# Three sums in another order, one more buffer, and two moved steps in a planned graph-network kernel

## Chip, cores and metric

The kernel runs on one core of one Trainium2 chip. The metric is the device time of one execution in microseconds (us). The kernel before took 2420.64 us in the median of three runs (2420.32 to 2423.39); the execution that the profiler recorded took 2417.17 us.

## What is computed

There are 128 graphs of 128 nodes with 512 features each. Two layers follow each other, both with a residual sum and a layer norm; all is float32.

```python
# layer 0: graph attention with 8 heads of 64 units
feats = einsum('bnf,hfu->bhnu', X, W)
dense = leaky_relu(e_self[..., :, None] + e_neigh[..., None, :], 0.2)
att = softmax(dense + NEG_BIG * (1.0 - A), axis=-1)
out = relu(einsum('bhij,bhju->bhiu', att, feats) + b)
x = layernorm(x + out)
...
# layer 1: hypergraph convolution, twice, with the incidence H = (adj != 0)
w = adj[:, 0, :]                       # the first row of the adjacency
Dn = 1 / einsum('nce,ne->nc', H, w)    # node scale
Be = 1 / H.sum(axis=1)                 # edge scale
conv(x, W) = Dn * (H @ (Be * (H.T @ (x @ W.T)))) + b
h = layer_norm(relu(conv(x, W1)))      # 512 -> 1024
y = conv(h, W2)                        # 1024 -> 512
x = layernorm(x + y)
```

## The kernel before

**Pairs and stages.** The work goes in 64 pairs of graphs (`PAIRS`), `p` from 0. Each pair passes through stages that are spread over five periods (`lag` 0 to 4): loads and masks first, then the features of the attention, the attention itself, the hidden layer h, and the output. In a steady period the engines work on several pairs at once, each in another stage.

**The order of the work is written by hand.** Every step has a planned time inside a period of `T = 38.6` planned units: `at(lag, time, fn, ...)` puts a step at `(p + lag) * T + time`. All steps of all pairs, and those of the prologue in `todo` (L1138), are sorted by this time (L1232) and issued in that order. So a planned time sets only the order in which an engine, or a DMA queue, gets its instructions. The tables `first` (L1161) and the one for the last pairs (L1219) give single steps other times. Each engine takes its instructions strictly in this order, and waits by itself where data or a buffer isn't ready. PE is TensorE, DVE is VectorE, ACT is ScalarE, POOL is GpSimd, and SP is SyncE, which issues most DMAs.

**Seven products instead of eight.** The three large multiplications (`chain`, L325: pf are features, ph the hidden layer, py the output) multiply blocks of two by two with seven products, which need sums of blocks of both operands. PE takes the products in the order 1, 2, 6, 5, 7, 4, 3. Products 1, 6, 7 and 4 add up in bank X, 2 in bank Y, 5 and 3 in bank W. ACT copies X after products 1, 6 and 7 into the buffers 0, 1 and 2 (`copy`, L340; the pf and py copies share buffers), and the results are sums of such a copy and Y or W: `f_sum` (L502), `h_sum` (L862) and `y_sum` (L925). Product 3 adds to W, so it waits until the DVE sum that reads W after product 5 is done.

**The h sums.** For py, the operand sums are made by POOL from h: `h_sums` (L909) calls `first_sums` (L458), one instruction of 128x512 each. With h[g] the halves of graph g of the pair:

```python
        in0, in1, op = (
            (a[1][0], a[1][1], ALU.add), (t[:, 0], a[0][0], ALU.subtract),
            (a[0][0], a[1][0], ALU.subtract), (a[0][1], t[:, 1], ALU.subtract),
        )[i]
```

Sum 0 takes h alone, sum 1 takes sum 0, sum 2 takes h alone, and sum 3 takes sum 1. Before the change POOL makes them in the order 2, 0, 1, 3. In `rows_product` (L479) product 6 takes sum 1, product 7 sum 2, product 5 sum 0 and product 3 sum 3. On POOL, `rstds` "o" and the three `squares` of graph 0 (L899) stand ahead of them, and the three `squares` of graph 1 behind. On PE, product 6 of py (planned 27.7) stands right behind `attend_pair` (L692, 64 small matmuls into pav), which multiplies the transposed attention eT. Half of eT is made by the second pair of `e_transpose` (L635) on DVE, planned at 21.5 and 21.55.

**The f sums.** Three of the four `f_sum` steps are on DVE: (0, 0) adds copy 0 and Y (planned 18.2), (1, 1) adds copy 2 and W (21.4), (0, 1) adds copy 1 and W after product 3 (24.4). (1, 0) is an ACT copy of X. Between 18.2 and 21.4 DVE has no other step.

**The first rows.** `load_first_row` (L108) brings w, the first row of the adjacency of both graphs, spread over all partitions, with two DMAs on SP. `nodes` (L353) multiplies it in place on DVE and writes node scales by way of `dn` and `dr`; `write_nodes` (L371) stores `dr` to DRAM (`dd_d`) and `spread_nodes` (L572) reads it back spread (`dnb`), for `r_evict` (L448, R). The tile w has one buffer. In the prologue `load(3)` is planned at 143.1, and `nodes` of pair 2 at 149.8, so that the load of pair 3's w stands in the SP queue before the step that uses pair 2's. Behind it on SP stand `load_rows` (x), `write_sums`, `read_sums` (149.77), `write_nodes` and `spread_nodes` of pair 2.

**The squares' sums.** The variance of h is summed over the partitions by way of DRAM: `sum_blocks` (L946, DVE) makes `sr`, `write_sums` and `read_sums` store it (`sd`) and read it back (`sums_out`), and `sum_rest` (L971, DVE) adds the rest. `h_rstd` (POOL, L997) makes the scale of `y_scale` (DVE, L1004), and `output` (PE, pq) follows it.

**The weight sums of the prologue.** `second_sums` (L221) makes four sums of blocks of W2 once. t1 and t2 are POOL's (planned 126.5), t3 (`slice(2, 3)`, b22 - b12) is DVE's at 123.15, t4 DVE's at 141.0. Around t3 on DVE stand `r_evict` of pair 1, a maximum of pair 1, `h_sum` (1, 1) of pair 0 (126.55) and `scale_edges` of pair 2 (126.6).

Of the kernel before, what the change touches and what calls it, by code (L numbers as in the profile page):

```python
# [8 lines left out]
F32 = mybir.dt.float32  # L9
# [11 lines left out]
def kernel(  # L21
# [45 lines left out]
    nc = tc.nc  # L67
    G, N, F = x.shape
    P = 128
# [14 lines left out]
    work = ctx.enter_context(tc.tile_pool(name="work", bufs=1))  # L84
# [22 lines left out]

    def load_first_row(p):  # L108
        s = st[p]
        s["w"] = work.tile([P, 2, N], F32, tag="w", name=f"w_{p}")  # L110
        for g in range(2):
            nc.sync.dma_start(s["w"][:, g, :], adj[2 * p + g, 0, :].partition_broadcast(P))

    def load(p):
        load_adj(p)
        load_first_row(p)
# [195 lines left out]
    LAST = PAIRS - 1  # L312
# [9 lines left out]
    def at(lag, time, fn, *args, since=0, until=PAIRS):  # L322
        steps.append((lag, time, fn.__name__, range(since, until), fn, args))
# [168 lines left out]
    def feature(s, i, to, start):  # L492
# [4 lines left out]
          feature, FW, since=2)  # L497
# [9 lines left out]
        else:  # L507
            nc.vector.tensor_tensor(dst, by_head(s["pf", i]), by_head(s["pf", where]), op=ALU.add)

    at(1, 18.2, f_sum, 0, 0, 0, "Y", since=2)  # L510
    at(1, 21.4, f_sum, 1, 1, 2, "W", since=2)
    at(1, 24.4, f_sum, 0, 1, 1, "W", since=2)
    at(1, 23.4, f_sum, 1, 0, None, "X", since=2)
# [395 lines left out]
    def h_sums(p, s, i):  # L909
        first_sums(s, "hS", f"hS_{p}", halves(s["h"], KH // 2), i, nc.gpsimd, "hS")  # L910

    at(3, 20.9, h_sums, 0, until=LAST)
    at(3, 22.2, h_sums, 1, until=LAST)
    at(3, 19.6, h_sums, 2, until=LAST)
    at(3, 23.4, h_sums, 3, until=LAST)


# [1 line left out]
    def weigh(s, i, to, start):  # L919
# [3 lines left out]
          QU, 1, until=LAST)  # L923
# [198 lines left out]
    for t, fn, *args in (  # L1122
# [18 lines left out]
        (13.05, prepare_vectors, ()),  # L1141
        (14.05, load_weights, (nc.scalar, w1_blocks[:2], w1t, F // 2, HALF)),
        (12.95, load_first_row, (1,)),
        (15.46, load_weights, (nc.sync, w1_blocks[:1:-1], w1t, F // 2, HALF)),
        (16.1, everywhere, (b2_bc, b2, nc.sync)),
# [7 lines left out]
        (117.8, prepare_output_blocks, (slice(2, 3),)),  # L1153
        (118.1, prepare_output_blocks, (slice(3, 4),)),
        (126.5, prepare_output_block_sums, (nc.gpsimd, slice(0, 2))),
        (123.15, prepare_output_block_sums, (nc.vector, slice(2, 3))),
        (141.0, prepare_output_block_sums, (nc.vector, slice(3, 4))),
        (100.0, prepare_mean_columns, ()),
    ]
# [116 lines left out]
```

## Time and profile before

| what | value |
|---|---|
| median of three runs | 2420.64 us (2420.32 to 2423.39) |
| profiled execution | 2417.17 us |
| its span, first to last instruction | 2415.4 us |
| granted TensorE clock, mean over the span | 0.997 |
| one steady period, from product 6 to product 6 of the next pair (1223.26 to 1259.96) | 36.70 us |
| busy in a steady period (1186.57 to 1223.26): PE, DVE, POOL, ACT | 36.59, 32.22, 28.48, 23.73 us |
| PE busy in the first 150 us | 127.61 us |
| PE busy in the last 116 us | 105.65 us |
| HBM | 142 GB/s over the span |

A group of instructions in the profile is named by line, engine, operation and the tiles that it writes and reads (`pyX<-w_sb,hS`: product into py's bank X, from weights and h sums). PE is the matmul side of TensorE and PEld its weight loads, which overlap the matmuls; their ends are modelled, so that a PE "busy" without a gap can hide a short stall, and the distance from start to start is the better measure. Nearly all PE work has line 97, the helper `columns`, so groups are told apart by their tiles. "idle" in a timeline is the time in which the engine did nothing before the group, and the name behind it is what ended this. SPq is the queue of SP: its times are those at which DMAs are issued, not those at which they land.

### The profile page before, as it was taken

The numbers are of one execution on the slowest core, as the hardware profiler recorded it, in microseconds if no ns is written. First come the engines' busy times: TensorE is split into PE (matmuls) and PEld (weight loads), VectorE is DVE, ScalarE is ACT, GpSimd is POOL, SyncE is SP. The second block draws the span as 40 slices with busy tenths as digits, with TensorE's granted clock in tenths as the row PEclk, the third lists the DMA queues.
The fourth block names the chain that finished last, engine by engine and source line by source line (L and its number), as shares of the span: only waits on it lengthen the run. The fifth ranks groups of instructions, "written<-read, shape, count | busy, mean of one in ns | idle before, by whom it ended". The sixth has DMA issues, their size and how long they took to land.

```text
span 2415.4 us, 81039 instructions
## 1 busy us (share of the span) xinstructions
PE 2374.1 (98%) x32309; PEld 1880.3 (78%) x32309; DVE 2083.3 (86%) x4456; ACT 1524.0 (63%) x4481; POOL 1830.5 (76%) x2060
## 2 busy tenths in 40 slices
PE   7899999999999999999999999999999999999998
PEld 5677887877877878778878778778777777787776
DVE  7888889889888888898898898898888888888875
ACT  4565765756756656657657567567566576575663
POOL 5787787787777777877877877877778777777774
PEclk9999999999999999999999999999999999999999
DMA  6445545445455555454455454555554545545541
GB/s 196 131 132 157 146 142 155 139 143 153 148 144 148 147 147 149 142 154 143 139 154 147 140 151 145 143 149 146 149 147 141 153 141 140 149 139 147 149 120 45
DMA packets 432872, 347.10 MB, mean 144 GB/s; under 512 B 153176, under 2 KB 382064, under 8 KB 432496
## 3 DMA queue, kind: packets, MB, share of 16 engines
q1 hardware_dynamic: 429024, 337.46, 48.5%
q8 instruction: 255, 4.18, 0.7%
q10 hardware_dynamic: 3472, 4.47, 0.6%
q14 instruction: 121, 0.99, 0.2%
HBM read 239.08 MB, written 102.73 MB: 142 GB/s over the span
## 4 chain that ended last, share of the span: by engine, by line
PE 49%; DVE 22%; POOL 16%; DMA 5%; ACT 4%; issue 2%; SPq 1%; POOLq 0%; DVEq 0%; ACTq 0%
PE pyX L97 13%; PE phX L97 9%; POOL hS L468 8%; PE pyW L97 8%; POOL sq L903 5%; DVE o L804 4%; PE pz L97 4%; PE phY L97 4%; PE pyY L97 4%; DVE h L865 3%; DVE statso L758 2%; ACT nb L604 2%; DVE o L1023 2%; DVE hB L434 2%; DVE nm L610 1%
## 5 line engine op out<-in xcount | busy, mean ns | idle before, releaser
L343 ACT COPY py<-pyX 128x257 f32<-128x257 f32 x189 | 70.8, 374 | 540.2 <-PE pyX L97 523.8
L97 PEld LDWEIGHTS phX<-zS,w_sb 128*64 128x64 f32 x6144 | 345.1, 137 | 40.5 <-POOL ft L741 21.0
L97 PE MATMUL phX<-zS,w_sb 128*64 128x128 f32 x6144 | 368.5, 273 | 3.5 <-ACT ph L343 3.5
L903 POOL TENSOR_TENSOR sq<-sq 128x512 f32<-128x512 f32 (+2 forms) x384 | 344.3, 897 | 20.1
L588 POOL TENSOR_TENSOR nb<-nb,neg 128x512 f32<-128x512 f32 x256 | 320.3, 1286 | 29.9 <-DMA nb<-rd 29.0
L604 ACT ACTIVATE nb<-nb,ft 128x128 f32<-128x128 f32 x1020 | 325.3, 392 | 17.9 <-POOL nb L588 17.7
L618 ACT ACTIVATE nb<-nb,nm 128x128 f32<-128x128 f32 x1024 | 319.6, 390 | 12.1 <-DVE nm L610 12.0
L766 POOL TENSOR_TENSOR rso<-veo,mhalf 128x2 f32<-128x2 f32 x63 | 44.2, 702 | 337.9 <-DVE veo L764 337.9
L97 PE MATMUL pyX<-w_sb,hS 128*64 128x257 f32 x2016 | 243.3, 382 | 7.2 <-POOL hS L468 1.7
L97 PE MATMUL pyX<-w_sb,h 128*64 128x257 f32 x2016 | 240.3, 379 | 0.5 <-ACT py L343 0.5
L880 ACT ACTIVATE h<-h,vecs 128x128 f32<-128x128 f32 x768 | 239.1, 393 | 2.4 <-DVE h L865 1.7
L97 PE MATMUL pyW<-w_sb,hS 128*64 128x256 f32 x2016 | 239.5, 379 | 0.0
L610 DVE TENSOR_REDUCE nm<-nb 128x4 f32<-128x512 f32 x256 | 175.3, 685 | 41.0 <-ACT nb L604 38.3
L741 POOL TENSOR_TENSOR ft<-ft,b_bc 128x512 f32<-128x512 f32 x128 | 200.7, 1588 | 5.2 <-ACT ft L532 5.2
L97 PEld LDWEIGHTS pyX<-w_sb,h 128*64 128x64 f32 x2016 | 146.0, 137 | 73.9 <-ACT py L343 0.9
L97 PEld LDWEIGHTS pyW<-w_sb,hS 128*64 128x64 f32 x2016 | 144.4, 136 | 73.9 <-issue 0.3
L97 PEld LDWEIGHTS pyX<-w_sb,hS 128*64 128x64 f32 x2016 | 139.5, 136 | 79.8 <-POOL hS L468 15.2
L639 DVE STREAM_TRANSPOSE eT<-eb 128x512 f32<-128x512 f32 x252 | 163.7, 686 | 1.3 <-DMA eb<-ed 0.8
L1006 DVE SCALAR_TENSOR_TENSOR y<-y,rsh,bw_bc 128x512 f32<-128x512 f32 x126 | 150.1, 1229 | 13.7 <-POOL rsh L1002 13.7
L891 ACT ACTIVATE sq<-h 128x512 f32<-128x512 f32 x256 | 160.6, 628 | 2.1
L468 POOL TENSOR_TENSOR hS<-h 128x512 f32<-128x512 f32 x126 | 159.0, 1281 | 0.0
L804 DVE SCALAR_TENSOR_TENSOR o<-y,b_bc 128x512 f32<-128x512 f32 x128 | 158.5, 1277 | 0.0
(178 smaller groups left out, 5563.2 us busy)
## 6 DMA issues: line engine op xcount, KB each, us to landing
nb<-rd SPq DMA_DIRECT2D x127, 512.0 KB
ed<-nb SPq DMA_DIRECT2D x126, 512.0 KB
eb<-ed SPq DMA_DIRECT2D x504, 128.0 KB
x<-in_x_dram SPq DMA_DIRECT2D x64, 512.0 KB
out_dram<-o SPq DMA_DIRECT2D x63, 512.0 KB
xb<-in_x_dram SPq DMA_DIRECT2D x248, 128.0 KB
a<-in_adj_dram SPq DMA_DIRECT2D x64, 128.0 KB
w<-in_adj_dram SPq DMA_DIRECT2D x128, 64.0 KB
```

Source lines behind the costliest of these rows:

```text
L97: nc.tensor.matmul(to[rows], lhs[:, rows], rhs, start=start, stop=stop, skip_group_check=True)
L468: engine.tensor_tensor(t[:, i], in0, in1, op=op)
L588: nc.gpsimd.tensor_tensor(t, t, neg[:, :, None, :].to_broadcast([P, NB, HH, B]), op=ALU.add)
L604: nc.scalar.activation(t, t, AF.Prelu, bias=s["ft"][:, g, h, 0:1], alpha=SLOPE)
L610: nc.vector.tensor_reduce(s["nm"][:, g, hs], scores(p, s, g, hs).rearrange("p b h j -> p h b j"), AX.XY, ALU.max, negate=True,)
L618: nc.scalar.activation(t, t, AF.Exp, bias=s["nm"][:, g, h:h + 1])
L639: nc.vector.transpose(s["eT"][:, g, hs, :].rearrange("p h (b i) -> p h b i", b=NB), s["eb", g][:, :, hs, :].rearrange("p b h j -> p h b j"),)
L741: nc.gpsimd.tensor_tensor(t, t, b0_bc.rearrange("p (h u) -> p h u", h=H), op=ALU.add)
L804: nc.vector.scalar_tensor_tensor(s["o"][:, g, :], s["y"][:, g, :], 2.0, b2_bc, op0=ALU.mult, op1=ALU.add)
L880: nc.scalar.activation(dst[:, k, :], src[:, k, :], AF.Relu, bias=b1_sb[:, c:c + 1])
L891: nc.scalar.activation(s["sq"][:, g, q * KH // 2:(q + 1) * KH // 2, :], hid(s, g, q), AF.Square, scale=DH ** -0.5,)
L903: nc.gpsimd.tensor_tensor(t[:, :n, :], t[:, :n, :], t[:, n:2 * n, :], op=ALU.add)
```

## The change

Four edits; none changes what is computed, and no instruction is added or taken out.

1. The h sums get planned times so that POOL makes them in the order 0, 1, 2, 3 instead of 2, 0, 1, 3.
2. The tile w has two buffers instead of one (one more KB in each partition).
3. `f_sum` (0, 0) moves from 18.2 to 21.45, so that on DVE it comes right after `f_sum` (1, 1) instead of right before it.
4. t3 of the weight sums moves from 123.15 to 126.57, behind `h_sum` (1, 1) of pair 0 and ahead of `scale_edges` of pair 2.

```diff
-        s["w"] = work.tile([P, 2, N], F32, tag="w", name=f"w_{p}")
+        s["w"] = work.tile([P, 2, N], F32, tag="w", name=f"w_{p}", bufs=2)
...
-    at(1, 18.2, f_sum, 0, 0, 0, "Y", since=2)
+    at(1, 21.45, f_sum, 0, 0, 0, "Y", since=2)
     at(1, 21.4, f_sum, 1, 1, 2, "W", since=2)
     at(1, 24.4, f_sum, 0, 1, 1, "W", since=2)
     at(1, 23.4, f_sum, 1, 0, None, "X", since=2)
...
-    at(3, 20.9, h_sums, 0, until=LAST)
-    at(3, 22.2, h_sums, 1, until=LAST)
-    at(3, 19.6, h_sums, 2, until=LAST)
+    at(3, 19.6, h_sums, 0, until=LAST)
+    at(3, 20.9, h_sums, 1, until=LAST)
+    at(3, 22.2, h_sums, 2, until=LAST)
     at(3, 23.4, h_sums, 3, until=LAST)
...
-        (123.15, prepare_output_block_sums, (nc.vector, slice(2, 3))),
+        (126.57, prepare_output_block_sums, (nc.vector, slice(2, 3))),
```

## Prediction

> **What bounds the kernel now.** I read the page first, then the list of waits, then each engine's timeline over one steady pair of graphs (1200 to 1260 us), then the same over the prologue (0 to 160 us). The page shows TensorE (PE) busy nearly all the time, and yet its chain of waits spends half the span elsewhere:
>
> ```profile
> PE 2374.1 (98%) x32309; PEld 1880.3 (78%) x32309; DVE 2083.3 (86%) x4456; ACT 1524.0 (63%) x4481; POOL 1830.5 (76%) x2060
> PE 49%; DVE 22%; POOL 16%; DMA 5%; ACT 4%; issue 2%; SPq 1%; POOLq 0%; DVEq 0%; ACTq 0%
> ```
>
> A chain that leaves PE and comes back has to return through a PE wait, however short. The list of waits (total us, times, longest) names it; the second line matters further down:
>
> ```profile
> PEld pyX L97 <- POOL hS L468: 15.2, 58, 0.3
> DVE so L973 <- DMA sums_out<-sd: 63.8, 38, 4.0
> ```
>
> The timelines (start, length, work, count, idle before) place it. PE's weight load first, GpSimd's (POOL) sums second:
>
> ```profile
> 1220.90 2.12 PEld L702 LDWEIGHTS pav<-ft,eT 128*64 128x64 f32 x64
> 1223.26 1.50 PEld L97 LDWEIGHTS pyX<-w_sb,hS 128*64 128x64 f32 x16 [0.25 <-POOL hS L468]
> ```
> ```profile
> 1219.34 2.51 POOL L468 TENSOR_TENSOR hS<-h 128x512 f32<-128x512 f32 x2
> 1221.93 1.28 POOL L468 TENSOR_TENSOR hS<-hS,h 128x512 f32<-128x512 f32 x1
> ```
>
> The first two POOL sums are 2 and 0, the third is sum 1, which product 6 takes. It ends at 1223.21, and PE begins to load it at 1223.26. In pair 0 the sum was just in time, and nothing was lost:
>
> ```profile
> 73.47 2.14 PEld L702 LDWEIGHTS pav<-ft,eT 128*64 128x64 f32 x64
> 75.50 1.53 PEld L97 LDWEIGHTS pyX<-w_sb,hS 128*64 128x64 f32 x16
> ```
>
> From load to load this is 2.03 us in pair 0 and 2.36 in the steady pair: the wait costs **0.33 us**, its 0.25 plus the overlap with the work ahead that is lost. The matmuls agree: attention product, then product 6, from start to start 1.86 + 1.75 us in pair 0, 2.14 + 1.80 steady, again 0.33. All other groups of the steady period follow each other at one fixed distance in nearly every pair (36.70 us from pair to pair). So PE bounds it, with one hole per pair.
>
> The prologue has a larger hole. SyncE's queue and PE there:
>
> ```profile
> 78.91 0.37 SPq L106 DMA_DIRECT2D a<-in_adj_dram  x1
> 87.02 1.27 SPq L112 DMA_DIRECT2D w<-in_adj_dram  x2
> 88.81 0.47 SPq L959 DMA_DIRECT2D sd<-sr  x1
> 93.89 2.67 SPq L965 DMA_DIRECT2D sums_out<-sd  x4
> 96.66 0.38 SPq L373 DMA_DIRECT2D dd_d<-dr  x1
> 98.59 0.38 SPq L575 DMA_DIRECT2D dnb<-dd_d  x1
> ```
> ```profile
> 104.55 3.35 PE L97 MATMUL pq<-y,R 128*64 128x512 f32 x8 [4.12 <-DVE y L1006]
> ```
>
> The load of w for pair 3 stands from 79.3 to 87.0, until `nodes` of pair 2 (VectorE, DVE, 85.14 to 86.99) is done with the only buffer. Behind it wait the squares' sums (`sd`, ready at 85.21) and all that follows them.
>
> **What the Trainium skill says.** "TensorE: Matmul & The Clock Gate", section "What a matmul computes" and its table, lets PE pull weight loads ahead of running matmuls; the trace agrees (loads start 0.08 to 0.1 us before the loads ahead end, and the wait removes this). The same page, "Part 1: The HAM clock gate", has PE at half clock after about 3.4 us of idleness; here too: pq takes 3.35 us after 4.12 idle, 1.89 in the steady pair. "DMA: Bandwidth & Descriptors", section "Anatomy of one DMA", says that waits are held by the issuing sequencer, and that completion costs about 2 us: SP's stall above is such a wait, and dd_d, issued at 96.66, frees DVE at 98.67, 2.0 us later.
>
> **The change, part by part.**
>
> (1) Order of the h sums. Nothing is added; three POOL instructions change places inside an unbroken run, so what stands before and behind them keeps its time. Sum 1 moves from third to second, 1.28 us earlier; sum 2 moves to third and ends at 1223.2, while product 7 that takes it starts at 1226.80, or 1226.47 with the hole gone: 3.2 us spare. The margin at product 6 becomes 1.28 - 0.33 = 0.95 us. Next late is DVE: the second transposes (L639) end at 1220.95, the attention product starts at 1221.12. In pair 0 they ended 0.07 before its start, with no loss; where they were later (pair 53, 0.19 us after the start), its fifth matmul started 0.145 us after their end, and its undisturbed place is 0.115 after the start. So up to 0.03 before the start is free: the margin is 0.17 - 0.03 = **0.14 us**. It is needed only if DVE doesn't follow PE; but DVE's run up to there starts from PE's ph products (ACT's copy at 1204.66), so it moves along. Gain 58 x 0.33 = **19.1 us** (58 times in the list of waits). Pair 62 already has the order 0, 1, 2.
>
> What is taken back: the trip of the squares' sums through DRAM. From the end of L954 to L973 it takes 6.25 to 10.48 us over the 62 pairs; where above 8.74, the pair grew by just the excess (9.37: 37.33 us; 10.48: 38.44). The hole lies inside this allowance, so it shrinks to 8.74 - 0.33 + 0.14 = 8.55. Summed over the trips, the excess rises from 7.4 to 9.3 us: 2.0. In some ten of the same pairs the mask additions wait for nb (24 waits, 29.0 us) and push ACT's copies of zT; I put 0.1 each, 1.0. Together **-3.0**; the bounds are 0 (these pairs overlap) and -6 (each counted twice).
>
> (2) Two buffers for w. In steady pairs w is free 27 us of planned time before its next load: nothing. In the prologue w of pair 3 goes out at 79.3, the x load behind it at 80.3, sd at 85.24 instead of 88.81. The later pairs with slow DMAs had some 4.6 us from sd to the first read: read at 89.8, four of them to 92.4; dd_d at 92.4 instead of 96.66, dnb at 94.4 instead of 98.59. So the wait of `nodes` 3 for dd_d (3.68 us) goes, L973 comes at 95 instead of 98.88, and R, which waits for dnb until 103.25, at 99.0. y_scale then ends near 100.2, as PE ends product 7 (98.48 + 1.75 = 100.2): pq starts at 100.3 instead of 104.55. PE isn't idle for 4 us any more and keeps its clock, another 1.4. Next late is ACT's third ph copy, behind DVE's maxima: product 4 at 102.8 instead of 107.71. DVE, 4.2 to 4.7 us earlier, sets the attention product of that pair. I take **4.5**; 2.0 if sd's trip stays slow behind the x load (its write is 5 us behind it), 5.7 if DVE's waits all close. Not below nothing: no transfer is added, and each is issued earlier.
>
> (3) f sums swapped on DVE. The one for W runs 0.34 us earlier, the one for Y (0.41 us) as much later. PE takes W again at 1220.23, with the sum done at 1219.74: no wait now. Where DVE is late (pairs with 0.33 us at this place) the transposes behind the sums, not moved, are late as well, so the attention product gives the gain back. Cost: ACT's py copy, which takes the buffer that the Y sum reads, starts at about 1219.80 instead of 1219.56; the ft copy behind it waits 0.52 for PE, which covers it. Without that cover, 0.24 per pair. I take **0**, bounds -1 and +1 for all pairs.
>
> (4) The weight sum (L225, 1.28 us on DVE at 61.42) goes behind one h_sum, and PE's third product, which waits 1.54 us for that h_sum, starts 1.2 earlier. But ACT, full from 61.5 to 69, sets when pf is copied; PE waits there again (69.26, 0.38 now). ACT's own shift is 0.1. I take **0**, bounds 0 and +0.3. t3 is first needed by product 7, 15 us later.
>
> Sum: 19.1 - 3.0 + 4.5 = **20.6 us**. The profiled execution took 2417.17 us (span 2415.4): 2396.6. The median of the three runs is 3.5 above it, so 2420.6 - 20.6 = **2400**.
>
> **Rivals.** (A) Part of the hole moves to the next late engine. If DVE's transposes don't come with PE, the hole shrinks by their margin alone: 58 x 0.14 = 8.1, with 4.5: 2408. For it: 0.14 us is little. Against: the chain above ties DVE to PE. (B) The reorder doesn't do what it says, as another sum or another wait ends at the same time; only the prologue gains: 2416. Against: sum 0 and sum 1 both come earlier and POOL has no idle time in the run. (C) Slower: the sums' trip through DRAM becomes the bound. In the last eleven pairs before 2301 us trips averaged 9.2 us, 0.75 us each above the allowance of 8.55. If all 60 were so, 45 us would be paid instead of 7.4: 38 - 23.6 = +14, 2435. It decides from 41 such pairs of 60 on ((23.6 + 7.4) / 0.75); there were eleven. The timed runs' 3 to 6 us above the profiled one may be four to eight more of them.
>
> **How the numbers follow.** About 0.2%, 4.8 us, is what can be told from no change. Forecast 0.73, its own range 2392 (5.7 in the prologue, nothing taken back, 1 from the swap: 25.8, and 3 for the spread of runs) to 2406 (-6, 2.0, -1: 14.1). A 0.19, B 0.05, C 0.03. Reaching into A gives 2392 to 2409. Faster 0.92 (forecast and A), same 0.05 (B), slower 0.03 (C).
>
> **What would show it.** (1) No PEld wait on hS; 36.37 us from pair to pair; the chain almost all PE. (2) w at 79 us behind a; pq in the prologue without idle time and under 2 us long. (3) ACT's py copy 0.2 later, its ft copy unmoved. (4) PE's third product earlier, and a longer wait after it. I am wrong if PE's period stays above 36.5 in the pairs from 400 to 1800 us, or if the sums' trips grow.

## The result and the profile after

The changed kernel takes 2392.13 us in the median of four runs (2391.45 to 2395.00). The kernel before, run beside it on the same chip, takes 2420.48 us (four runs, 2420.04 to 2423.39). The ratio is 0.9883, with a 95% interval from 0.9865 to 0.99: **28.35 us faster**, where 20.6 us and 2400 us were forecast. The profiled execution of the changed kernel took 2395.00 us, with a span of 2393.2; before it was 2415.4. So the two profiled executions lie 22.2 us apart. The remaining 6 us lie between the profiled executions and the other runs: before, the median stands 3.3 us above the profiled one, and after, 2.9 us below it.

The page of the changed kernel, busy times and the chain of work that ended last:

```profile
PE 2359.4 (99%) x32309; PEld 1986.4 (83%) x32309; DVE 2079.3 (87%) x4456; ACT 1529.5 (64%) x4481; POOL 1827.5 (76%) x2060
PE 81%; DMA 7%; DVE 5%; ACT 2%; POOL 2%; SPq 2%; issue 1%; DVEq 0%; POOLq 0%; ACTq 0%
```

The chain now stays on PE for 81% of the span instead of 49%. PE was busy 98% of the time already, so this number could not show the hole. The share of the chain could.

The list of waits of the changed kernel (total us, times, longest) has no line any more in which PE's loads wait for the h sums. The first line below is new in its size (12.2 us before), the second was 63.8 us before, the third 29.0:

```profile
ACT py L343 <- DVE ft L508: 65.9, 58, 1.4
...
DVE so L973 <- DMA sums_out<-sd: 49.0, 36, 3.4
...
POOL nb L588 <- DMA nb<-rd: 30.4, 25, 5.1
```

The steady period of the changed kernel, POOL's sums and then PE's weight loads (start, length, work, idle before):

```profile
1213.61 1.28 POOL L468 TENSOR_TENSOR hS<-h 128x512 f32<-128x512 f32 x1
1214.97 1.27 POOL L468 TENSOR_TENSOR hS<-hS,h 128x512 f32<-128x512 f32 x1
1216.20 1.28 POOL L468 TENSOR_TENSOR hS<-h 128x512 f32<-128x512 f32 x1
1217.44 1.28 POOL L468 TENSOR_TENSOR hS<-h,hS 128x512 f32<-128x512 f32 x1
```
```profile
1215.16 2.14 PEld L702 LDWEIGHTS pav<-ft,eT 128*64 128x64 f32 x64
1217.19 1.53 PEld L97 LDWEIGHTS pyX<-w_sb,hS 128*64 128x64 f32 x16
```

Sum 1 is the second line and ends at 1216.24. Product 6 begins to load it at 1217.19, 2.03 us behind the load of the attention product, the distance that pair 0 had before. The margin is 0.95 us. From pair to pair it is 36.367 us in the median of the start-to-start distances, instead of 36.705. Taken from group to group on PE, in the median of 38 steady pairs, the attention product is 0.28 us shorter and product 6 0.05 us; every other distance is the same to 0.003 us.

The prologue of the changed kernel, SP's queue and then PE:

```profile
80.14 0.37 SPq L106 DMA_DIRECT2D a<-in_adj_dram  x1
80.56 1.92 SPq L112 DMA_DIRECT2D w<-in_adj_dram  x2
...
86.57 0.33 SPq L959 DMA_DIRECT2D sd<-sr  x1
89.65 2.66 SPq L965 DMA_DIRECT2D sums_out<-sd  x4
92.42 0.38 SPq L373 DMA_DIRECT2D dd_d<-dr  x1
93.90 0.38 SPq L575 DMA_DIRECT2D dnb<-dd_d  x1
```
```profile
101.58 1.92 PE L97 MATMUL pq<-y,R 128*64 128x512 f32 x8
```

The load of w goes out right behind that of a, `sd` 2.2 us earlier than before although this run reached product 6 of pair 0 1.3 us later, and pq follows without idle time in 1.92 us instead of 3.35. The granted clock of PE, recorded as 0.5 from 104.0 to 107.4 us before, is 1.0 there now. From product 6 of pair 0 to that of pair 1 it takes 40.30 us, before 45.77.

**Where the 22.2 us went**, in sums worked out from the starts in the trace: 60 periods of 0.338 us less are 20.3; the first period, from product 6 of pair 0 to that of pair 1, is 5.5 shorter; the pairs that run longer than the median cost 9.7 us beyond it instead of 7.4 (I call this their excess), so -2.3; and the run reached product 6 of pair 0 1.3 us later (76.89 against 75.55), so -1.3. Together 22.2.

### The profile page after: what moved, and what is told of

It is laid out like the page before. It is cut to its first block, busy times and chain, and to the rows that moved or that the text cites. A ratio compares the mean times of both kernels' runs of the same rounds, so it can differ in the third digit from the quotient of the medians.

```text
span 2393.2 us, 81039 instructions
## 1 busy us (share of the span) xinstructions
PE 2359.4 (99%) x32309; PEld 1986.4 (83%) x32309; DVE 2079.3 (87%) x4456; ACT 1529.5 (64%) x4481; POOL 1827.5 (76%) x2060
## 3 DMA queue, kind: packets, MB, share of 16 engines
q8 instruction: 256, 4.19, 0.7%
## 4 chain that ended last, share of the span: by engine, by line
PE 81%; DMA 7%; DVE 5%; ACT 2%; POOL 2%; SPq 2%; issue 1%; DVEq 0%; POOLq 0%; ACTq 0%
PE phX L97 16%; PE pyX L97 15%; PE pfX L97 8%; PE phW L97 8%; PE pyW L97 7%; PE phY L97 4%; PE pq L97 4%; PE pfW L97 4%; PE pav L702 4%; PE pz L97 4%; PE pyY L97 4%; DMA nb<-rd 3%; PE pfY L97 2%; DMA rd<-rows 1%; DMA ed<-nb 1%; ACT nb L604 1%
## 5 line engine op out<-in xcount | busy, mean ns | idle before, releaser
L604 ACT ACTIVATE nb<-nb,ft 128x128 f32<-128x128 f32 x1020 | 325.1, 392 | 19.4 <-POOL nb L588 19.4
L97 PEld LDWEIGHTS pyX<-w_sb,h 128*64 128x64 f32 x2016 | 166.4, 136 | 53.5 <-ACT py L343 0.9
L97 PEld LDWEIGHTS pyW<-w_sb,hS 128*64 128x64 f32 x2016 | 168.1, 136 | 50.1 <-issue 0.3
L97 PEld LDWEIGHTS pyX<-w_sb,hS 128*64 128x64 f32 x2016 | 161.9, 136 | 43.8
L804 DVE SCALAR_TENSOR_TENSOR o<-y,b_bc 128x512 f32<-128x512 f32 x128 | 164.0, 1320 | 0.0
```

What stands on the lines that cost most here:

```text
L97: nc.tensor.matmul(to[rows], lhs[:, rows], rhs, start=start, stop=stop, skip_group_check=True)
L604: nc.scalar.activation(t, t, AF.Prelu, bias=s["ft"][:, g, h, 0:1], alpha=SLOPE)
L804: nc.vector.scalar_tensor_tensor(s["o"][:, g, :], s["y"][:, g, :], 2.0, b2_bc, op0=ALU.mult, op1=ALU.add)
```

## The experiments

The theory was the prediction's, and the rivals were those of the prediction and, later, several on the pairs that run longer. All times are medians, and each ratio is to the kernel before on the same chip, in the same set of runs: 2425.16 us for e1 to e4, 2427.88 for e5 to e8, 2427.28 for e9 to e12.

### One part at a time

**e1_h_order_only**: of the change, only this.

```diff
-    at(3, 20.9, h_sums, 0, until=LAST)
-    at(3, 22.2, h_sums, 1, until=LAST)
-    at(3, 19.6, h_sums, 2, until=LAST)
+    at(3, 19.6, h_sums, 0, until=LAST)
+    at(3, 20.9, h_sums, 1, until=LAST)
+    at(3, 22.2, h_sums, 2, until=LAST)
```

> Of the four edits only the order of the h sums (0, 1, 2, 3). Theory (the hole of 0.33 us per pair at product 6 is the main gain): 36.37 us from pair to pair in undisturbed pairs, no PEld wait on hS, 18 to 22 us faster than before, no gain in the prologue, where SP still waits until 87 us with the load of w. Rival (a good part of the 28 us comes from the swapped f sums or the moved weight sum): less than 15 us faster.

Measured: 2404.86 us, 0.9916 (0.9901 to 0.9931), 20.3 us faster. The period is 36.367 us. The hole of the prologue is still there, and larger in this run:

```profile
106.77 3.68 PE L97 MATMUL pq<-y,R 128*64 128x512 f32 x8 [5.58 <-DVE y L1006]
```

So the order makes the whole of the steady gain by itself.

**e2_w_buffers_only**: of the change, only `bufs=2` for w.

```diff
-        s["w"] = work.tile([P, 2, N], F32, tag="w", name=f"w_{p}")
+        s["w"] = work.tile([P, 2, N], F32, tag="w", name=f"w_{p}", bufs=2)
```

> Of the four edits only the two buffers for w. Theory: about 5 us faster, all of it before 125 us: pq of the prologue starts without idle time; the steady period stays at 36.70 us. Rival (what is won in the prologue is lost again at the next wait on hS): 0 to 2 us.

Measured: 2418.61 us, 0.9975 (0.9965 to 0.9985), 6.5 us faster. The period stays at 36.70, and PE's line at the same place of the prologue is

```profile
100.75 1.92 PE L97 MATMUL pq<-y,R 128*64 128x512 f32 x8
```

**e3_f_swap_only**: of the change, only this.

```diff
-    at(1, 18.2, f_sum, 0, 0, 0, "Y", since=2)
+    at(1, 21.45, f_sum, 0, 0, 0, "Y", since=2)
```

> Of the four edits only the two f sums swapped. Theory: within 1 us of before; ACT's py copy starts about 0.24 us later, nothing else moves. Rival (the swap shortens the DMA trips of late pairs, as PE's product 3 isn't held and the spread rows go out earlier): 2 to 6 us faster.

Measured: 2425.70 us, 1.0005 (0.9995 to 1.0015). PE's loads for bank W of the features wait 1.2 us in all (5 times, 0.2 at most) instead of 3.6 (8 times, 0.6 at most), and the attention product waits for DVE instead (1.8 us, 6 times; the list of before has no such wait).

**e4_t3_moved_only**: of the change, only this.

```diff
-        (123.15, prepare_output_block_sums, (nc.vector, slice(2, 3))),
+        (126.57, prepare_output_block_sums, (nc.vector, slice(2, 3))),
```

> Of the four edits only the weight sum t3 moved behind one h_sum. Theory: within 0.5 us of before, as PE's third product starts 1.2 us earlier and PE then waits as much longer for ACT's pf copies. Rival: 1.2 us faster.

Measured: 2426.90 us, 1.0005 (0.9996 to 1.0013). PE's third product starts without a wait, and then PE waits 0.47 and 0.48 us for two copies of pf: the gain is handed back at once.

The four parts give 20.3 + 6.5 - 0.5 - 1.7 = 24.6 us, all together 28.4 and, measured again below, 29.8. The two parts that do nothing have 1 inside their intervals (2.0 to 2.4 us to each side), so this is additive to within a few us.

### Is it the order, and what is the next margin?

**e5_sum1_third**: the changed kernel, but POOL makes the sums in the order 0, 2, 1, 3. Sum 1 is third again, with another sum ahead of it.

```diff
-    at(3, 20.9, h_sums, 1, until=LAST)
-    at(3, 22.2, h_sums, 2, until=LAST)
+    at(3, 22.2, h_sums, 1, until=LAST)
+    at(3, 20.9, h_sums, 2, until=LAST)
...
-                    ("squares", 0): 26.5, ("squares", 1): 26.6, ("h_sums", 2): 22.3,
+                    ("squares", 0): 26.5, ("squares", 1): 26.6, ("h_sums", 2): 22.1,
```

> The changed kernel with the h sums in the order 0, 2, 1, 3: sum 1 is third again, as before the change, and the other three edits stay. Theory (only the place of sum 1 counts): the PEld wait on hS is back with about 0.25 us in each pair, the period is 36.70 us again, some 20 us slower than the changed kernel (5 to 7 us faster than before). Rival (it was the early sum 2 that cost something, or the run as a whole): within 5 us of the changed kernel.

Measured: 2416.66 us, 0.9959 (0.9944 to 0.9974), some 20 us slower than the changed kernel by the ratios (0.9878 for e9 below). The period is 36.588 us, not the 36.70 that had been expected: 0.12 us of the hole are missing, and of the expected waits of 0.25 us in each pair the list shows 21, of 0.2 us at most. The loads in this kernel's steady period:

```profile
1218.03 2.12 PEld L702 LDWEIGHTS pav<-ft,eT 128*64 128x64 f32 x64
1220.28 1.50 PEld L97 LDWEIGHTS pyX<-w_sb,hS 128*64 128x64 f32 x16
```

From load to load it is 2.25 us, between the 2.03 without a hole and the 2.36 with it. In the order 2, 0, 1 sum 1 reads what the instruction right ahead of it wrote, and POOL starts it 0.07 to 0.08 us after that one's end (1214.89 to 1214.97 in the lines after, where the independent sum behind it starts 0.04 us before the end). In the order 0, 2, 1 there is one instruction between the two. So the place of sum 1 makes most of the hole and its dependence on its neighbour the rest. Both point to sum 1 and to no other wait. Of the 20 us, 60 periods of 0.22 us make 13; most of the rest is the excess of the longer pairs (15.5 us against 10.0 in e9), which has another cause, shown below.

**e6_pool_spare_256** and **e7_pool_spare_512**: the changed kernel with one more POOL addition ahead of the h sums of each pair, with 256 columns in the first and 512 in the second. Its result is not used.

```diff
+    spare = const.tile([P, F], F32, name="spare")
+
+    def extra(p, s, engine, n):
+        engine.tensor_tensor(spare[:, :n], b0_bc[:, :n], b2_bc[:, :n], op=ALU.add)
+
+    at(3, 19.5, extra, nc.gpsimd, 256, until=LAST)
```

> The changed kernel with one spare GpSimd addition of 128x256 (about 0.7 us) in each pair ahead of the h sums; its result is used by nothing. Theory (margin of 0.95 us at product 6): no PEld wait on hS, period 36.37 us, within 3 us of the changed kernel. Rival (the margin isn't there): 0.3 us or more per pair, 18 us.

> The same with a spare addition of 128x512 (about 1.27 us), again used by nothing. Theory: 1.27 - 0.95 = 0.32 us beyond the margin, so that the wait of before is back: period 36.69 us, about 19 us slower than the changed kernel. Rival (margin larger, or the spare work falls into POOL's idle time): period 36.37 us.

Measured: 2397.26 us, 0.9874 (0.9858 to 0.9891), and 2413.52 us, 0.9941 (0.9926 to 0.9956). With 256 columns POOL comes 0.73 us later, the period is 36.374, and PE does not wait. With 512 columns it comes 1.275 us later, and the old hole is back. The waits and the loads of e7:

```profile
PEld pyX L97 <- POOL hS L468: 15.4, 58, 0.4
```
```profile
1222.80 2.12 PEld L702 LDWEIGHTS pav<-ft,eT 128*64 128x64 f32 x64
1225.16 1.50 PEld L97 LDWEIGHTS pyX<-w_sb,hS 128*64 128x64 f32 x16 [0.24 <-POOL hS L468]
```

Again 2.36 us from load to load, and a period of 36.707. Of the 1.275 us, 0.34 reach PE, so the margin was 1.275 - 0.34 = 0.93 us, where the prediction had 0.95. By the ratios e7 is some 15 us slower than the changed kernel (0.9941 against 0.9878), where 19 had been expected; its excess is smaller, 7.6 us.

**e8_dve_spare_264**: the changed kernel with the same kind of spare addition on DVE, ahead of the second transposes of eT, to measure the margin of 0.14 us there.

```diff
+    at(1, 21.46, extra, nc.vector, 264, since=3)
```

> The changed kernel with one spare DVE addition of 128x264 (about 0.34 us) in each pair from pair 3 on, between the f sums and the second transposes of eT; its result is used by nothing. Theory (DVE's margin at the attention product is 0.14 us): PE waits there for DVE eT, the period grows by 0.34 - 0.14 = 0.20 us to 36.57, 12 us in all. Rival (DVE has no margin): 0.34 us, 20 us. Second rival (DVE has the same slack as POOL): nothing.

Measured: 2452.45 us, 1.0104 (1.0089 to 1.0119); the period is 37.43 us, 1.06 more, where 0.20 had been expected. That was a miss in the size of the probe. All of the 1.06 us stands in the attention product; every other distance on PE is that of the changed kernel to 0.001 us. DVE, PE and POOL of this kernel at the same moment:

```profile
1199.62 0.42 DVE L508 TENSOR_TENSOR ft<-pf,pfY 128x264 f32<-128x264 f32 x1
1199.96 1.24 DVE L912 TENSOR_TENSOR spare<-b_bc 128x264 f32<-128x264 f32 x1
1201.13 1.29 DVE L639 STREAM_TRANSPOSE eT<-eb 128x512 f32<-128x512 f32 x2
```
```profile
1202.57 1.97 PE L702 MATMUL pav<-ft,eT 128*64 128x65 f32 x60 [0.84 <-DVE eT L639]
```
```profile
1199.65 1.27 POOL L468 TENSOR_TENSOR hS<-h 128x512 f32<-128x512 f32 x1
1200.99 1.35 POOL L468 TENSOR_TENSOR hS<-hS,h 128x512 f32<-128x512 f32 x1
```

The f sum has the same 264 columns, with one operand in PSUM, and takes 0.42 us. The spare has both in SBUF and takes 1.24: it starts at 1199.96 inside a POOL sum that runs to 1200.92, and ends some 0.3 us after it. The Trainium skill says this in "SBUF — State Buffer", section "Who interferes with whom": a DVE instruction with two SBUF inputs contends with a GpSimd instruction that reads SBUF; the ports that the two share are held by one of them at a time, and the order of issue decides which one is blocked. The trace agrees: in all 61 pairs the spare takes 1.23 to 1.25 us and ends 0.29 us after that POOL sum. The transposes came 1.17 us later (1201.13 after 1199.96) and PE lost 1.06, so the margin is 1.17 - 1.06 = 0.11 us, against 0.14 in the prediction.

### The pairs that run longer

In some pairs the step from SP's write of `rd` to the read `nb` behind it takes over 2.2 us, mostly 2.5 to 3.5, instead of 1.5; I call them late pairs. What they cost, and what the trip of the squares' sums costs beside them, is the term of the sum that did not come as said. First, is it the traffic beside them?

**e9_changed_again** (the changed kernel, no edit) and **e10_ab_early** (the same, with `load_edges` of the later pairs at another place in the SP queue):

```diff
-            todo.append((p * T + (28.5 if p == 2 else 20.5), load_edges, (p,)))
+            todo.append((p * T + (28.5 if p == 2 else 20.5 if p == 3 else 0.1), load_edges, (p,)))
```

> The changed kernel once more, as the measure of the three kernels beside it. Theory: 27 to 33 us faster than before; the pairs that take longer than 36.37 us are again among the first fifteen, and in each of them one 16 KB packet of the instruction queue starts within 1.4 us after the issue of the spread rows' write (rd<-rows).

> The changed kernel with load_edges (ab, 1024 packets of 128 B a pair) issued from pair 4 on at the start of the period, behind w, and not just ahead of rd<-rows. Theory (rd's write stands behind ab's packets): the time from rd's issue to the issue of nb falls from 1.5 to 1.0 us or less in quiet pairs, late pairs lose less, 3 to 8 us faster than the changed kernel. Rival (completion alone makes the 1.5 us, the instruction packets the rest): within 2 us of it.

Measured: 2397.49 us, 0.9878 (0.9865 to 0.9891), and 2397.97 us, 0.9883 (0.9870 to 0.9896). As expected, e9 is 27 to 33 us faster than before, and the longer pairs are mostly the early ones: of 15 pairs over the median 12 are among the first thirteen, all of them late, each with a packet of the instruction queue 0.5 to 1.5 us after the issue of `rd`. Moving the kernel's own load away from `rd` (e10) does nothing that can be told: the quiet step stays at 1.43 us and more, where 1.0 had been expected, so the rival came. e10 has fewer late pairs, and PE waits for DVE's transposes eight times instead, 9.8 us in all, which wait for a DMA.

The trace's single DMA packets point elsewhere. The page counts 256 packets on a queue that no line of the kernel uses:

```profile
q8 instruction: 256, 4.19, 0.7%
```

4.19 MB in 256 packets are 16 KB each, and each takes about 1.0 us. Where such a packet starts between 0 and 1.0 us after `rd` is issued, the pair was late in 132 of 132 cases, over the first ten profiles (before, after and e1 to e8). With none from 1.5 us before to 1.7 us after it, the pair was late 13 times of 321. The same two SP instructions in the changed kernel, in a late pair and in a quiet one:

```profile
374.54 0.40 SPq L551 DMA_DIRECT2D rd<-rows  x1
378.00 0.94 SPq L569 DMA_DIRECT2D nb<-rd  x2
```
```profile
1216.41 0.34 SPq L551 DMA_DIRECT2D rd<-rows  x1
1217.86 1.76 SPq L569 DMA_DIRECT2D nb<-rd  x2
```

From issue to issue 3.46 and 1.45 us. If PE's own instruction stream is what these packets carry, more PE instructions early in the program must move them against the work.

**e11_pe_64_ahead** and **e12_pe_192_ahead**: the changed kernel with 16 (48 in the second) calls of `columns` more in the first pair, each of four small matmuls, whose results are overwritten.

```diff
+        if p == 0:
+            for _ in range(16):
+                columns(s["px"][0][:, :64], ident, ident[:, :64], True, True)
```

> The changed kernel with 16 spare products (64 PE instructions, loads and matmuls) in the prologue while PE waits for the first x; they are overwritten and used by nothing. Each PE instruction block of 16 KB (256 instructions) is then fetched some 2.3 us earlier in the pair. Theory (an instruction packet that starts between rd's issue and 1.4 us later makes the pair late): the packets of the first fifteen pairs move ahead of rd's issue and those of the others come to -0.9 to 0 us; the late pairs change their places altogether. If packets up to 1 us ahead of rd's issue count too, nearly all pairs become late, and it is 10 to 30 us slower than the changed kernel; if not, it is up to 10 us faster. Rival (lateness comes from the data in flight or from the place in the run): the same pairs are late, within 2 us of the changed kernel.

> The same with 48 spare products (192 PE instructions). The packets come 6.8 us earlier, which puts the following one 2.3 us later than before: 3 us and more after rd's issue in all pairs. Theory: hardly a late pair, 5 to 10 us faster than the changed kernel, with the PE period at 36.37 us from pair 2 on. Rival: as for the kernel with 64: the same pairs are late, within 2 us.

Measured: 2431.47 us, 1.0019 (1.0010 to 1.0029), and 2437.48 us, 1.0038 (1.0025 to 1.0051). The work added at the start delays product 6 of pair 0 by 1.2 and 4.8 us, and yet the kernels are **34 and 40 us slower** than e9. Their runs scatter more, too, from 2419.8 to 2438.5 us. The median period is 37.05 and 36.97 us. Both moved the packets, but e12 should have been fast, so this expectation failed. The waits of e11, whose lines stand three further down in the file:

```profile
DVE so L976 <- DMA sums_out<-sd: 139.2, 60, 4.2
POOL nb L591 <- DMA nb<-rd: 88.1, 65, 4.9
PEld phX L97 <- ACT zT L831: 23.6, 39, 1.4
```
```profile
1230.48 0.40 SPq L554 DMA_DIRECT2D rd<-rows  x1
1233.26 0.94 SPq L572 DMA_DIRECT2D nb<-rd  x2
```

56 of 62 pairs are late in e11 and 54 in e12, against 15 in the changed kernel. The cause of the miss is in the counts of the records: 64 matmuls are **128** instructions, since each has its weight load, and 192 are 384. Both are half a block of 256 (384 = 256 + 128), so the two experiments set the same phase, the place of the block boundary against the work. Other phases were not tried, and neither was a whole block of 256 more, which would leave the phase alone and show what the spare work costs by itself.

Counted this way all 14 profiles fall into line. The Trainium skill, "Runtime: NRT & Kernel Launch", section "Instruction fetch mechanics", says that each engine fetches its program in 16 KB blocks of 256 instructions through a DMA queue of its own. The trace agrees: 65537 PE records of the changed kernel in 256 packets, 65920 of e12 in 257. That section calls the cost of a block boundary mostly hidden; the late pairs here speak against it for a DMA beside the fetch. Take for each pair the count of PE's records ahead of `rd`'s issue, modulo 256. At 144 to 255 and 0 to 15, 234 of 249 pairs are late; at 48 to 127, 21 of 430; between them it is mixed.

Now the counts of the kernels. A steady pair has 1021 PE records before and **1022** after the change. The additional one is a wait: 916 semaphore instructions on PE instead of 854, 62 more. Before, sum 2 stood ahead of sum 1 on POOL, so product 6's wait for sum 1 covered product 7's sum 2. In the new order product 7 needs a wait of its own. Four blocks are 1024, so the phase falls by 3 per pair before and by 2 after. Both start between 156 and 170. Before, the count runs down past 48 and over zero to 244 by the last pair, after, it ends at 49:

| kernel | PE records per pair | count at the first and the last pair | late pairs of 62 |
|---|---|---|---|
| before, e2, e3, e4, e5 | 1021 | 156 to 170, 244 | 22, 23, 24, 26, 24 |
| after, e1, e6, e7, e9 | 1022 | 156 to 170, 49 | 15, 15, 17, 16, 16 |
| e8, e10 (DVE or SP work moved beside `rd`) | 1022 | 158 and 156, 21 and 49 | 7, 10 |
| e11, e12 | 1022 | 27 and 29, 176 | 56, 54 |

e7 has the long period of before but the order of after, and stands with the latter, so the late pairs go with the count and not with the length of the period. That the block fetch delays `rd` is a correlation over 868 pairs, together with two kernels in which little but the count moved; it is not isolated further. Why the zone lies where it does, and why e8 and e10 escape part of it, is open.

Where does PE pay for late pairs? Against the median distances of the changed kernel, PE loses 40 us in e11 over 60 pairs: 21 in front of the first product of the hidden layer (41 pairs), where it waits for zT, its operand, which ACT copies out of PSUM; ACT waits for `nb` by way of POOL (48.6 us in e11, 19.4 in the changed kernel). Another 14 us stand in the attention product, and 3 in front of pq and right behind it. In the changed kernel itself 6.3 of 9.3 us stand in front of that first product, in nine pairs, of which eight are late ones.

## Why the prediction was right, and which terms were off

**Bound and mechanism: right.** One hole per pair in an otherwise full PE, in front of product 6, and one hole in the prologue. e1 and e2 close one each.

**(1) Order of the h sums: right, with one fact missed.** Predicted 19.1 us, measured 20.3, alone and in the profile: the wait was listed 58 times at 0.33, while 60 periods are 0.338 shorter. The margin of 0.95 us was measured as 0.93 (e7), and that of DVE, 0.14, as 0.11 (e8), under a delay larger than was meant. DVE did move along with PE, so rival A (2408) did not come, and e1 alone excludes rival B (2416). The text said that no instruction is added. On POOL this holds; on PE 62 wait instructions are added.

**What is taken back: the step that failed.** I put -3.0. Between the two profiled executions -2.3 came, and that it is so close is luck, for its parts are off. The trips of the squares' sums beyond 8.55 us were to add up to 9.3 us; they add up to 3.8 (pair 0 left out), so they shrank where I had named growth as a sign of being wrong. ACT's copies of zT, which I had priced at 1.0, held PE up by 6.3 us. And e1, e6 and e9 show an excess of 13.7, 12.9 and 10.0 us, and e2, e3 and e4, where the period did not shrink, 13.4, 13.4 and 15.1. So between runs of the same kind nothing is taken back in sum. Two things work against each other. A shorter period seems to cost something: e7 has the late pairs of after (16) but the period of before, and its excess is 7.6 us, against 9.7 to 13.7 in after, e1, e6 and e9; this is one profile. But the late pairs fell too, from 22 to 26 down to 15 to 17, since, by the counts above, the additional wait keeps the kernel out of the last late stretch. The prediction held the number of late trips fixed, and took the profiled execution of before (7.4) as typical, which has the smallest excess of all the profiles with its order of the sums.

**(2) Two buffers for w: right, undersized.** Predicted 4.5, bounds 2.0 to 5.7. Measured 6.5 (e2), and 5.47 less the 0.34 of the h sums, so 5.1, between the profiled executions. Counted from product 6 of pair 0, pq starts 4.29 us earlier (4.25 predicted), and from pq to the product behind it PE takes 1.45 us less (1.4 predicted). The prediction then took 1.2 of these 5.7 off again, since DVE would set the attention product of the next pair. DVE does: the loads behind the fourth begin 0.12 us after the end of its transposes. But PE loses 0.55 us there (2.41 us to product 6 instead of 1.86). This is the term that was mis-sized. DVE may have been earlier because `sd` to its read took 3.1 us instead of the 4.6 that I took from the later pairs with slow DMAs. Also, the hole of before was not always 4.12 us: in e1, e3 and e4, with one buffer, it is 5.50 to 5.63 us and pq takes 3.68. From product 6 to product 6 the kernels with one buffer take 45.8 to 48.2 us, those with two 40.3 to 42.0. The profile had caught the mildest case.

**(3) f sums: right.** ACT's py copy now starts 0.62 us before its ft copy instead of 0.89, so 0.27 later (0.24 predicted), and the ft copy still waits 0.25 us for PE. That is the wait of 65.9 us (12.2 before) in the list above. It is the largest new line of the profile, and it costs nothing that can be told: e3 has it too, with 65.7 us, at 1.0005.

**(4) t3: right.** PE's third product waits 0.24 us for DVE's h_sum instead of 1.54, then 0.68 and 0.48 us for the pf copies; e4 by itself can't be told from before (1.0005).

**Rival C (slower, from 41 late trips of 60): not here.** e11 and e12, with 56 and 54 pairs late at `rd`, are slower than before, so that the danger was real. It came from the place of the instruction blocks, which the prediction had not seen, and in the main by another path than rival C had it: the trips of the squares' sums beyond 8.55 us add up to 23 us in e11, but only 3 us of what PE loses stand at pq, which needs these sums. How much of the 14 us in the attention product comes from them by way of DVE is not separated.

**The total.** Between the profiled executions 20.3 + 5.5 - 2.3 - 1.3 = 22.2 stands against 19.1 + 4.5 - 3.0 = 20.6. The other 6 us lie in runs without a profile. More late pairs and a longer first hole there before the change would explain them, and this is not shown; the profiles of e3 and e4, which time like before, do have a first period longer by 1.7 to 2.4 us and an excess larger by 6.0 to 7.7 than the profile of before.

**How close it was.** The measured 2392.13 us lies at the very edge of the predicted 2392 to 2406, and e9, measured beside before once more, is faster by 29.8 us, which is more than the range allows. The 25.8 us of its fast end hold 1 us from the swap, which gave nothing, and its last 3 us were for the spread of runs. So the mechanism of the two main parts is shown, while the hit of the range owes something to luck.

## What to carry to other kernels

When an engine is busy 98% of the time and yet the chain keeps leaving it, look for one short wait that recurs: measured from start to start it costs more than the idle time shown (0.25 shown, 0.34 paid), and the order of the producer's instructions can remove it without any work less. Before such an edit, measure the next margin with a spare instruction on the producer, as e7 does, and mind that a probe can be dearer than what it imitates (e8). Differences of 1% and more between kernels in which only a few instructions move (34 and 40 us of 2397 here) can go with where the instruction blocks fall against a short DMA round trip: count instructions per period modulo 256 before you believe an explanation in terms of the work.

## What the hardware showed that I had not expected

- A 16 KB instruction packet takes about 1.0 us, and where one starts within 1.0 us after the issue of a short write to DRAM, the step to the read behind it is longer by some 1.0 to 2.0 us (132 of 132 cases). With 56 of 62 pairs late the kernel is 34 us slower (e11 against e9).
- A different order of the same POOL instructions changes the number of PE's wait instructions, by one per pair (854 to 916).
- A DVE addition of 128x264 takes 1.24 us with both operands in SBUF beside a POOL addition, and 0.42 us with one of them in PSUM.
- A POOL addition of 128x512 that reads the result of the one right ahead of it starts 0.07 to 0.08 us after its end; an independent one starts 0.04 us before it.
- pq's eight matmuls of 512 columns take 3.68 us after 5.58 us of idleness (e1) and 1.92 us without it (e2).
